# A two-layer graph kernel on Trainium2: the adjacency of layer 0 turned from the float32 tile itself, the first score pieces filled a round early, second buffers for two tiles

## The chip, the cores and the metric

The kernel runs on one core of one Trainium2 chip. The metric is device time in microseconds (us) of one execution. The kernel before took 15358.9 us, the median of three runs (15358.85 to 15360.56).

A core has five engines with an instruction queue each: PE (TensorE, matrix products; PEld is its loading of the stationary operand), DVE (VectorE), ACT (ScalarE), POOL (GpSimd) and SP (SyncE, which here only issues transfers). Sixteen DMA engines move data between device memory, SBUF (the on-chip memory, 128 partitions) and DRAM scratch. Matrix products land in PSUM.

## The reference

Two layers over 3327 nodes with 128 features, and a 0/1 adjacency matrix of 3327 x 3327 in float32. Both layers add their result to their input and normalize.

```python
# layer 0: cosine attention over the neighbours
norm2 = jnp.linalg.norm(x, axis=1, keepdims=True)
cos = beta[0] * (x @ x.T) / (norm2 @ norm2.T + 1e-07)
masked = cos + (1.0 - adj) * -1000000000.0
x = _layernorm(x + jax.nn.softmax(masked, axis=1) @ x)

# layer 1: 128 small attentions, one for each feature d, with 8 columns per head matrix
q = (x @ Wq.T).reshape(d, n, h); k = ...; v = ...
a = jnp.einsum('dnh,dmh->dnm', q, k) * scale
a = jax.nn.softmax(a + adj + adj, axis=2)
out = jnp.einsum('dnm,dmh->dnh', a, v).reshape(n, h * d) @ Wo.T
x = _layernorm(x + out)
```

## The kernel before

The nodes are padded to 3328 = 26 tiles of 128 rows (`T` = 26, `NP` = 3328). Layer 0 goes row tile by row tile and takes some 800 us; layer 1, the long part, takes the rest. In both, the order of PE, ACT, DVE and POOL is the order of the program text (a manual schedule), so that an instruction that has to wait holds up all that stands behind it on its engine. SP also issues its transfers in the order of the text.

**A tile's way through layer 0.** `load(t)` brings the adjacency rows as float32 into `u.raw` (1663.5 KB, through SP's queue; three buffers, shared with layer 1's keys) and the rows of x into `u.xr`. `load_bits(t)` brings the same rows a second time, through POOL's queue, converted to bf16 into `u.bits` (two buffers). `adj_chunk(t, c)` turns four 128 x 128 blocks of `u.bits` by matrix products with a unit matrix (L396) into a PSUM tile `tp`, and ACT copies them into `u.aT` (L397, one buffer); after the seventh chunk `u.aT` goes out to the scratch `aT_s` (L399), which layer 1 reads. `inverse_log`, `inverse_exp`, `inverse_product`, `inverse_newton` (L410, L417, L424, L431) make the reciprocals of the products of norms in `u.y`, on ACT and DVE. `mask(t)` (L403, ACT) turns the adjacency in `u.raw`, in place, into 0 or -1e9. `scores(t, j)` handles one of four pieces of 832 columns: `score_piece` fills a PSUM tile `sc` (two buffers) with x @ x.T (L359, four matrix products on record), then DVE scales it (L441) and adds the mask and takes the running minimum (L444). `weights(t, i)` (L460, ACT) takes the exponential of half a row. `turn_weights(t, c)` turns four blocks of it on PE (L134) into `tp` (two buffers, shared with `adj_chunk`) and copies them out (L474 on DVE, L472 on ACT for chunks 5 and 6); `weigh0` multiplies them with x (L482). `norm_begin`, `norm_root`, `norm_end` normalize. `project_turn` and `project(t, k)`, k = 0 to 5, make q, k and v of layer 1: each is a product into the PSUM tile `pq` (one buffer, L533) that ACT copies out, for q and k into `row` (L549), which POOL splits into `high` (L554) and `low` (L555), two buffers each, that go to scratch (L558, `qn_s` and `kn_s`); for v into `nine` (L535, one buffer), which goes to the scratch `v_s` (L539).

**A round.** The loop over t runs rounds -2 to 28, each with eight steps k = 0 to 7. Round t holds the scores of tile t (k = 0 to 3), the weights, turns and weighing of tile t-1, the normalization of tile t-2, the projections of tile t-3 (k = 0 to 4), the reciprocals and the mask of tile t+1 (k = 1 to 6), the turned adjacency of tile t+2 (chunk 0 at k = 4, chunks 1 and 2 at k = 5, 3 and 4 at k = 6, 5 and 6 at k = 7), `load(t + 3)` at k = 5, and `load_bits(t + 4)` at the end. After rounds 8, 12, 16 and 20 `gather` copies finished q and k rows from scratch to scratch. From round 26 on the first part of layer 1's search for row maxima is mixed in (`first_max`), and it uses the same two `sc` buffers.

The order at the head of a round, k = 0, is what the change touches on PE, ACT and DVE:

```python
weights(t - 1, 0)
project(t - 3, 0)
norm_begin(t - 2)
scores(t, 0)
turn_weights(t - 1, 0)
weights(t - 1, 1)
project(t - 3, 1)
norm_root(t - 2)
```

## Time and profile before

| what | us |
|---|---|
| median of three runs | 15358.9 |
| the profiled execution, its own time | 15361.32 |
| its span, first to last instruction | 15359.5 |
| layer 0, to the first product of layer 1's main loop | some 821 |
| PE / DVE / POOL / ACT busy in the whole span | 15192.6 / 13818.7 / 13765.0 / 12755.2 |

The profile is of one execution. Its page gives the busy time of each engine, the span in slices, the transfers by queue, the chain of waits that ended last, and the costliest groups of instructions. The trace behind it can be asked for any stretch: busy times and the granted clock of PE, the list of instructions in order of time with the idle time ahead of each and what ended it, and the sum of waits by who waited for whom. Times inside the span count from its first instruction. Of a matrix product the end is modelled, so neighbouring products overlap on record.

Where the rounds of layer 0 lie, by the start of their first scaling of scores (L441, in us; the list of instructions gives them):

| round | 0 | 1 | 2 | 3 | 4 | 5 | 11 | 13 | 15 | 19 | 23 | 25 |
|---|---|---|---|---|---|---|---|---|---|---|---|---|
| start | 62.1 | 78.2 | 101.6 | 123.7 | 149.2 | 174.3 | 322.8 | 376.3 | 430.7 | 538.4 | 647.0 | 696.1 |

From round 5 to round 11 a round takes (322.8 - 174.3) / 6 = 24.75 us, from 11 to 25 (696.1 - 322.8) / 14 = 26.66 us.

### The profile page before, as it was taken

To read this page: it belongs to the slowest core of one execution; us is meant where nothing else is said; L and a number is where in the kernel's file an instruction comes from. 1 tells how busy PE (TensorE), PEld (TensorE's weight loads), DVE (VectorE), ACT (ScalarE), POOL (GpSimd) and SP (SyncE) were. 2 spreads that over 40 slices of the span, in tenths; PEclk is the share of its full clock that TensorE was granted. 3 is DMA by queue.
4 is the path that set the end of the run, shared out by engine and by line. 5 is a ranking of instruction groups with operands and counts; after the bars stand their busy time and mean duration, and the time that the engine had idled before them with its cause. 6 is when DMAs were issued, how large, how long until landed. Compare 5 with 4: busy or idle time off the path is not lost.

```text
span 15359.5 us, 494776 instructions
## 1 busy us (share of the span) xinstructions
PE 15192.6 (99%) x210460; PEld 6695.5 (44%) x210460; DVE 13818.7 (90%) x15851; ACT 12755.2 (83%) x25413; POOL 13765.0 (90%) x8979
## 2 busy tenths in 40 slices
PE   8899999999999999999999999999999999999999
PEld 5534444444444444444444444444444444444555
DVE  7889999999999999999999999999999999998776
ACT  7689998888888888888888888888888888888777
POOL 3389999999999999999999999999999999998887
PEclk9999999999999999999999999999999999999999
DMA  7732221111111111111111111111111111111112
GB/s 229 226 103 97 101 98 60 48 51 48 56 50 47 52 53 53 46 53 46 60 47 53 47 58 48 51 48 55 51 46 53 46 59 46 53 46 62 62 59 83
DMA packets 553135, 1018.81 MB, mean 66 GB/s; under 512 B 148711, under 2 KB 493284, under 8 KB 504582
## 3 DMA queue, kind: packets, MB, share of 16 engines
q1 hardware_dynamic: 547126, 965.00, 19.1%
q0 software_dynamic: 3792, 22.15, 0.8%
q8 instruction: 1648, 27.00, 0.7%
q14 instruction: 569, 4.66, 0.1%
HBM read 871.04 MB, written 192.54 MB: 69 GB/s over the span
## 4 chain that ended last, share of the span: by engine, by line
PE 96%; DMA 1%; DVE 1%; ACT 1%; issue 0%; SPq 0%; POOL 0%; DVEq 0%; ACTq 0%; POOLq 0%
PE acc L808 30%; PE ea L778 22%; PE m L262 16%; PE eb L791 13%; PE ea L791 10%; PE ea L797 1%; PE ea L764 1%; DMA aT_s<-aT 1%; PE eb L797 1%; PE acc L482 0%; PE pq L533 0%; PE sc L359 0%; ACT aT L397 0%; PE pp L993 0%; DMA qn_s<-high 0%
## 5 line engine op out<-in xcount | busy, mean ns | idle before, releaser
L899 POOL TENSOR_TENSOR pb<-pb,eT 128x768 f32<-128x768 f32 (+1 forms) x7488 | 13175.3, 1767 | 980.4 <-ACT pb L898 594.0
L277 DVE TENSOR_REDUCE mx<-m 128x2 f32<-128x1024 f32 x6753 | 8275.0, 1225 | 958.6 <-PE eb L797 555.4
L898 ACT ACTIVATE pb<-eb 128x768 f32<-128x768 f32 (+1 forms) x7488 | 5898.0, 788 | 2255.7 <-PE eb L797 1731.1
L262 PE MATMUL m<-kn,qx 32*128 32x512 f32 (+1 forms) x23128 | 6804.0, 471 | 0.1
L922 ACT ACTIVATE pa<-ea 128x384 f32<-128x384 f32 (+1 forms) x14976 | 6338.9, 478 | 23.0 <-PE ea L778 8.4
L808 PE MATMUL acc<-pb,vt 128*9 128x384 f32 (+1 forms) x29952 | 5903.7, 474 | 0.1
L808 PE MATMUL acc<-pa,vt 128*9 128x384 f32 (+1 forms) x29952 | 5903.7, 474 | 0.0
L298 DVE TENSOR_REDUCE mx<-m 128x1 f32<-128x512 f32 x6371 | 4338.5, 681 | 252.0 <-PE m L262 232.3
L791 PEld LDWEIGHTS <-one 3*128 3x128 bf16 x29952 | 1465.8, 91 | 5659.0 <-issue 4661.4
L778 PE MATMUL ea<-aT,two 128*32 128x384 bf16 (+1 forms) x59904 | 3715.6, 325 | 0.0
L797 PE MATMUL eb<-qx,kn 32*128 32x384 f32 (+1 forms) x13312 | 3030.2, 451 | 0.0
L797 PE MATMUL ea<-qx,kn 32*128 32x384 f32 (+1 forms) x13312 | 2938.7, 433 | 0.0
L262 PEld LDWEIGHTS m<-kn,qx 32*128 32x128 f32 x23128 | 2797.6, 182 | 216.3 <-DVE mx L298 4.7
L791 PE MATMUL ea<-cx,one 3*128 3x384 bf16 (+1 forms) x14976 | 2724.4, 324 | 0.2
L791 PE MATMUL eb<-cx,one 3*128 3x384 bf16 (+1 forms) x14976 | 2466.1, 326 | 16.9 <-ACT cx L869 16.7
L808 PEld LDWEIGHTS acc<-pa,vt 128*9 128x9 f32 x29952 | 1418.2, 91 | 399.9
L808 PEld LDWEIGHTS acc<-pb,vt 128*9 128x9 f32 x29952 | 1418.6, 91 | 387.0 <-issue 0.7
L778 PEld LDWEIGHTS <-two 128*32 128x32 bf16 x59904 | 938.1, 94 | 1421.5 <-issue 1231.0
L797 PEld LDWEIGHTS eb<-qx,kn 32*128 32x128 f32 x13312 | 1275.0, 188 | 0.0
L797 PEld LDWEIGHTS ea<-qx,kn 32*128 32x128 f32 x13312 | 1237.0, 182 | 8.0 <-issue 1.3
L302 DVE TENSOR_REDUCE mx<-m 128x2 f32<-128x512 f32 x1084 | 739.7, 682 | 20.3 <-PE m L262 19.1
L554 POOL CAST high<-row 128x512 fp32r<-128x512 f32 x104 | 96.0, 923 | 328.7 <-DMA qn_s<-high 209.9
(134 smaller groups left out, 5972.2 us busy)
## 6 DMA issues: line engine op xcount, KB each, us to landing
kn<-kp_s SPq DMA_DIRECT2D x512, 832.0 KB
vt<-v_s SPq DMA_DIRECT2D x288, 409.5 KB
kn<-kq_s SPq DMA_DIRECT2D x64, 832.0 KB
qx<-qp_s SPq DMA_DIRECT2D x1016, 48.0 KB
kn<-in_adj_dram SPq DMA_DIRECT2D x25, 1663.5 KB
qp_s<-qn_s SPq DMA_DIRECT2D x64, 416.0 KB
kp_s<-kx SPq DMA_DIRECT2D x32, 832.0 KB
kq_s<-kn_s SPq DMA_DIRECT2D x64, 415.9 KB
```

What stands on the lines that cost most here:

```text
L262: nc.tensor.matmul(dst, u.qx[rows(a), q * P : (q + 1) * P], u.km[rows(a), k0:k1], start=True, stop=True,)
L277: nc.vector.tensor_reduce(u.mx[:, h, qs[0], c], m, axis=AX.X, op=ALU.max)
L298: nc.vector.tensor_reduce(u.mx[:, a, qs[0], c : c + 1], m, axis=AX.X, op=ALU.max)
L302: nc.vector.tensor_reduce(u.mx[:, a, qs[0] : qs[1] + 1, c], m.rearrange("p (q k) -> p q k", q=2), axis=AX.X, op=ALU.max,)
L764: nc.tensor.matmul(dst[r], parts[u.i % 2][:, q, h], unit, start=start, stop=True, tile_position=(0, 32 * h), skip_group_check=True,)
L778: nc.tensor.matmul(e[r, : u.nq], two[:, r], aT[:, j, : u.nq], start=False, stop=True, tile_position=(0, 32 * c), skip_group_check=True,)
L791: nc.tensor.matmul(e[:, : u.nq], one[r], u.cx[r, : u.nq], start=True, stop=False, skip_group_check=True)
L797: nc.tensor.matmul(e[:, : u.nq], u.kx[rows(a), j * P : (j + 1) * P], u.qx[rows(a), : u.nq], start=False, stop=stop, skip_group_check=True,)
L808: nc.tensor.matmul(acc[32 * h : 32 * h + H + 1, : u.nq], u.vt[:, h, j], pts[h][:, : u.nq], start=(j == 0), stop=(j == T - 1), tile_positio ...
L898: nc.scalar.activation(pt_b[:, :, : u.nq], e_b[:, :, : u.nq], AF.Exp)
L899: nc.gpsimd.tensor_tensor(pt_b[:, :, : u.nq], pt_b[:, :, : u.nq], eT[:, j, : u.nq].unsqueeze(1).to_broadcast([P, 2, u.nq]), ALU.mult,)
L922: nc.scalar.activation(pt_a[:, h, : u.nq], e[:, : u.nq], AF.Exp)
```

## The change

All of it is in layer 0.

- The second load of the adjacency is gone (`load_bits`, with its memset of the pad column and its transfer on POOL's queue, and the pool that held `bits`). `adj_chunk` reads instead the upper 16 bits of each float32 word of `u.raw`, which for 0 and 1 are the same number in bf16. Within a partition its 128 elements lie 104 bytes apart, those of `bits` lay 52 bytes apart. `u.raw` of tile t+2 must now be there at k = 4 of round t, before `mask(t + 2)` overwrites it in round t+1; before, it was first read at k = 4 of round t+1.
- `u.aT` has two buffers, and so has `nine`.
- The matrix products of `scores` move into `fill(t, j)`: pieces 0 and 1 of tile t+1 are filled at k = 6 and k = 7 of round t, ahead of the adjacency chunks of those steps; piece 2 at the end of k = 0, piece 3 at the end of k = 1. DVE's part of `scores(t, 0)` moves ahead of `project(t - 3, 0)` and `norm_begin(t - 2)`.

```diff
-        def load_bits(t: int):
-
-            u = tiles[t]
-            u.bits = adj_raw.tile([P, NP], BF16, name="bits", bufs=2)
-            load_adj(u.bits, nc.gpsimd, t)
+        def upper(t: int, k: int):
+
+            halves = tiles[t].raw.bitcast(BF16)
+            return halves.rearrange("r (p t h) -> r t h p", t=T, h=2)[:, k, 1, :]
 
         def adj_chunk(t: int, c: int):
...
-                u.aT = ptp.tile([P, T, P], BF16, name="aT", bufs=1)
+                u.aT = ptp.tile([P, T, P], BF16, name="aT", bufs=2)
...
-                nc.tensor.matmul(tp[:, k - a], every(u.bits, k), unit, start=True, stop=True)
+                nc.tensor.matmul(tp[:, k - a], upper(t, k), unit, start=True, stop=True)
...
+        def fill(t: int, j: int):
+            if there(t):
+                tiles[t].sc[j] = score_piece(xT[:, t * P : (t + 1) * P], xT, j)
+
         def scores(t: int, j: int):
...
-            sc = score_piece(xT[:, t * P : (t + 1) * P], xT, j)
+            sc = u.sc.pop(j)
...
             if n == 2:
+                nine = nines[t % 2]
...
-            for t in range(2):
-                load_bits(t)
-            nine = big.tile([P, P, R9], F32, name="nine")
-            nc.gpsimd.memset(nine[:, :, H], 1.0)
+            nines = [big.tile([P, P, R9], F32, name=f"nine{i}") for i in range(2)]
+            for nine in nines:
+                nc.gpsimd.memset(nine[:, :, H], 1.0)
...
                     if k == 0:
                         if there(t - 1):
                             weights(t - 1, 0)
+                        if there(t):
+                            scores(t, 0)
                         if there(t - 3):
                             project(t - 3, 0)
                         if there(t - 2):
                             norm_begin(t - 2)
-                        if there(t):
-                            scores(t, 0)
                         if there(t - 1):
                             turn_weights(t - 1, 0)
                             weights(t - 1, 1)
...
                             norm_root(t - 2)
+                        fill(t, 2)
...
                     if k < 5 and there(t - 3):
                         project(t - 3, k + 1)
+                    if k == 1:
+                        fill(t, 3)
+                    if k >= 6:
+                        fill(t + 1, k - 6)
                     if k == 5 and there(t - 2):
                         project_turn(t - 2)
...
-                if there(t + 4) and t + 4 > 1:
-                    load_bits(t + 4)
```

More of the change, by code (lines that the diff above doesn't have):

```diff
@@ L345, in gnn_two_layers @@
         big = l0.enter_context(tc.tile_pool(name="l0_big", bufs=1))
-        adj_raw = l0.enter_context(tc.tile_pool(name="adj_raw", bufs=2))
         work = l0.enter_context(tc.tile_pool(name="l0_work", bufs=2))
@@ L368, in gnn_two_layers, with there @@
         tiles = [Tile0() for _ in range(T)]
+        for u in tiles:
+            u.sc = {}
+        def there(n: int):
+            return 0 <= n < T
         half = NP // 2
@@ L633, in gnn_two_layers @@
             for t in range(-2, T + 3):
-                def there(n: int):
-                    return 0 <= n < T
                 for k in range(8):
```

## The prediction, on record before the change was run

> **What bounds the kernel now.** First the page's chain of waits, shares by engine and by line.

> ```profile
> PE 96%; DMA 1%; DVE 1%; ACT 1%; issue 0%; SPq 0%; POOL 0%; DVEq 0%; ACTq 0%; POOLq 0%
> PE acc L808 30%; PE ea L778 22%; PE m L262 16%; PE eb L791 13%; PE ea L791 10%; PE ea L797 1%; PE ea L764 1%; DMA aT_s<-aT 1%; PE eb L797 1%; PE acc L482 0%; PE pq L533 0%; PE sc L359 0%; ACT aT L397 0%; PE pp L993 0%; DMA qn_s<-high 0%
> ```

> 96% is PE, nearly all of it in layer 1, which the change leaves alone. Only layer 0, some 821 us or 5%, can move, and it ends before layer 1 begins, so what it saves passes to the end. The 1% of `aT_s<-aT` is about 114 us of chain, but not a gain of 114 us: while the chain goes through it, the rounds take nearly the usual time. So I went on by busy times, two stretches of 25 us (then narrow ones around a stall); the last two columns are the DMA engines' share and GB/s, and the one before them the granted clock.

> ```profile
> 212.90:237.70 24.80, 22.77 (x133) 15.88 (x133) 22.43 (x32) 20.38 (x28) 9.43 (x11) 1.00 0.86 250
> 395.00:420.00 25.00, 20.65 (x106) 13.69 (x106) 17.92 (x29) 16.70 (x22) 8.73 (x11) 0.93 0.77 233
> 575.30:578.70 3.40, 1.64 (x12) 1.22 (x10) 3.40 (x4) 0.89 (x2) 0.00 (x0) 1.00 0.97 403
> 578.70:582.10 3.40, 3.40 (x14) 2.24 (x14) 3.37 (x3) 3.14 (x2) 0.00 (x0) 0.51 0.80 272
> 237.40:240.80 3.40, 1.98 (x12) 1.34 (x11) 3.40 (x5) 3.37 (x2) 0.19 (x2) 1.00 0.55 160
> ```

> A quiet round (first line) is nearly full on PE, DVE and ACT at once, and the DMA engines are 86% busy. In a disturbed one the clock falls too: 3.4 us in which PE was busy 1.64 are followed by 3.4 us at half clock, 3.4 us with 1.98 are not. Next the sums of waits, and the queues, both from 95 to 700 us.

> ```profile
> POOL high L554 <- DMA qn_s<-high: 207.8, 19, 21.0
> DVE s L441 <- PE sc L359: 52.4, 40, 6.8
> ACT row L549 <- POOL low L555: 12.0, 3, 4.2
> ACT aT L397 <- DMA aT_s<-aT: 9.9, 8, 1.9
> ACT nine L535 <- DMA v_s<-nine: 9.4, 3, 4.1
> ...
> q1 hardware_dynamic: 110238, 127.12, 62.7%
> q0 software_dynamic: 3072, 17.89, 17.0%
> ```

> Three rows are ACT stopped by a transfer, 31.3 us: its tile is still going out, or POOL waits for its own. q0 is the load of `bits`: 17.0 of 79.7 points.

> **The second load and the second buffers.** The disturbed rounds are late by (26.66 - 24.75) x 14 = 26.7 us, which fits those 31.3 us, part of them absorbed, with the half clock behind them. With two buffers the rows of `aT` and `nine` go. The 12.0 us of `row` go if transfers keep up: q1 alone is 63%, and a round's raw load, v and turned tile queue up together from round 9 on only because each round was 80 to 90% full. I take 25 us off; bounds 19 (the two rows alone, all of it direct) and 31.

> **The start.** PE waits for x until 15.50, POOL until 19.83.

> ```profile
> 15.50 1.94 PE L134 MATMUL tp<-ident,xn 128*128 128x128 f32 x8 [15.50 <-DMA xn<-in_x_dram]
> 19.83 5.73 POOL L603 TENSOR_TENSOR s<-xn 128x3328 f32<-128x3328 f32 x1 [15.74 <-DMA xn<-in_x_dram]
> ...
> 2.00:7.00 5.00, 0.00 (x0) 0.00 (x0) 0.00 (x0) 0.02 (x1) 1.74 (x4) 1.00 0.88 249
> 7.00:14.00 7.00, 0.00 (x0) 0.00 (x0) 0.00 (x0) 0.00 (x0) 0.00 (x0) 1.00 1.07 241
> ```

> x's first transfer is 1638 KB; from 2 to 7 us it moves 249 x 5 = 1245 KB alone, then `bits` of two tiles shares the engines to 16 us. Without them the other 393 KB take 1.6 us, not 7: 5.3 us off, and all behind it moves up, the raw loads too (issued at 15.5, right after). Bounds 0 (another limit on x) and 9.5 (2 x 831.8 KB at that rate is 6.7, plus the wait behind them).

> **The scores filled early, first rounds.** In rounds 0 and 1 no projection fills PE, and DVE waits for `sc` 3.00, 2.22 and 0.59 us there. Filling early takes most of it, but at half clock a fill takes 2.8 us and now stands ahead of the adjacency chunks: 4 us off, bounds 0 and 6.

> **The scores filled early, a full round.** Here I follow one round by the step from one start to the next in the list of instructions from 195 to 222 us.

> ```profile
> 196.77 1.08 PE L533 MATMUL pq<-wq,x1T 128*128 128x512 f32 x2
> 197.36 1.69 ACT L460 ACTIVATE s<-s,mn 128x1664 f32<-128x1664 f32 x1
> 197.68 1.56 PE L359 MATMUL sc<-xT 128*128 128x416 f32 x4
> 199.19 0.66 PE L134 MATMUL tp<-ident,s 128*128 128x128 f32 x4
> 199.28 1.08 DVE L441 SCALAR_TENSOR_TENSOR s<-sc,by_q,y 128x832 f32<-128x832 f32 x1 [0.99 <-PE sc L359]
> 215.89 0.58 ACT L535 COPY nine<-pq 128x512 f32<-128x512 f32 x1
> 218.67 0.44 PE L134 MATMUL tp<-ident,s 128*128 128x128 f32 x2 [0.41 <-ACT aT L397]
> 220.29 1.95 ACT L397 CAST aT<-tp 128x512 bf16<-128x512 f32 x4 [0.78 <-PE tp L396]
> ```

> Let 196.77, PE's first projection, be 0. The first turn waits for ACT's weights: 0.6 (ACT ends its adjacency copies) + 1.69 + 0.13 = 2.4. Before, 1.4 us of scores stood in that wait; now nothing, so PE idles 1.3 to 1.5 us. From there PE's steps are projection 0.9, fill 1.4, turn 0.44, weighing 0.9, projection 0.86, fill 1.4, then (turn 0.44, weighing 0.9, projection 0.86) for k = 2 to 4. DVE comes before each of them now: its waits at the first and fourth turned block, 0.6 and 1.0 us, are gone. But ACT has 16.6 us of its own from the weights on: weights 3.5, logarithm 3.06, exponentials 3.1, mask 3.0, four rows and two v copies 3.0, the rest 0.9. With 0.6 ahead and 0.4 of waits its second v copy ends at 17.6; before it ended at 19.7. Then adjacency copy, weights copy, x1T and another adjacency copy, 1.75 together, let the seventh turn begin at 19.4; before 21.9, so 2.5 us gained. Behind it stand turn 0.28, weighing 0.9, fill 1.4, chunks 0.5, weighing 0.55, fill 1.4, chunks 0.6 = 5.6: the next round begins at 25.0, against 24.75. The fills leave the head, where they covered ACT, for the tail, where PE alone sets the pace; DVE gets 2 us of idle time that nobody uses. So +0.3 us a round for 23 rounds: +7. Bounds per round: -1.9 (DVE's busy 22.43 and small gaps, 22.85, if ACT could keep up) and +1.5 (no wait of DVE's was on the path).

> **What else moves.** The raw load is issued at 216.92, 20.2 us into its round, and now first read at adjacency chunk 0 of the next one, some 23 us later; in quiet rounds its packets are through 6 to 9 us after the issue, and PE would wait only if SP fell more than 14 us behind. Behind SP's load stand x's rows, the turned tile and the next `high`. In rounds 9 to 23 SP did issue it 8 to 13 us later in the round; that lag came with POOL's 207.8 us of waits for `high`. I put this at 0; the cover is those 14 us. The weight loads read words 104 bytes apart instead of 52. The trace has no such load; the nearest rows are PE's load of `bits` itself, 157 ns median with 83 ns from start to start, and ACT's copies at a step of 104 bytes (L752, 452 ns) against one without (L525, 266 ns). Bounds 0 and 0.19 x 26 = 4.8 us a round; I take 0, as PE's own row is nearer. POOL's memsets and issues, 0.7 us a round, stood in its idle time: 0.

> **Sum.** -25 - 5.3 - 4 + 7 = -27.3. The profiled execution took 15361.3 (span 15359.5), so 15334; it lies 2.4 above the median, so the median should come to **15332**.

> **Rivals.** *PE's new idle time halves its clock* (slower side). The place is the first turn of each round: 3.4 us with 1.64 busy us are punished, with 1.98 not. An idle 1.5 plus 0.1 at the next projection leaves 1.8, between them. It decides once the idle time passes 1.7, which a late adjacency copy of 0.2 us would do. A window of 3.4 us holds the whole gap in some 0.55 of rounds; half clock for one window costs 1.7 us, for two (as after 367 us) 3.4: 23 x 0.55 x 1.7 = +22, or 15354, and at two windows +43, or 15375, slower than before. Against it: gaps of 1.42 and 1.43 us in rounds 3 and 7 cost nothing. [...]

> *DVE sets the pace.* If ACT's copies slip into PE's idle time better than my steps let them, the round falls to 22.85: (24.75 - 22.85) x 23 = -44 instead of +7, so 15281. For it: 52.4 us of DVE waits named. Against: ACT's 16.6 us in the head leave no room.

> *The raw load comes late.* If SP's lag of 13 us stays, PE waits perhaps 2 us a round in 14 rounds and the 25 us come back: 15361. Against: with q0 gone the queue drains in each round.

> *The wide stride costs.* At half the bound, 2.4 x 26 = +62: 15394. Against: the loads of `bits` already skip.

> **How the numbers follow.** My forecast 0.56, half clock 0.21 (a fifth of it past 15390), DVE's pace 0.11, raw load 0.07, stride 0.05. The range for 8 in 10 goes from 15300, between the forecast and DVE's pace, to 15366, above the one-window clock case and the raw load; the likeliest case's own is 15318 to 15348. What a measurement can tell from no change is 0.2%, 31 us, so 15328 divides. Of the forecast 0.27 lies below it; with DVE's pace 0.38 faster. Slower, above 15390: 0.04 of the clock and 0.05 of the stride, 0.09. Within: 0.53.

> **What would show it.** Right: no q0 bytes in layer 0, x at PE near 10 us, waits of `aT` and `nine` for transfers gone, rounds from 11 to 25 as long as those from 5 to 11 and both near 25.0, DVE idle some 2 us more, the first turn waiting 1.3 to 1.5 us for the weights. Wrong: rounds at 23, a clock below 1.00 in quiet stretches, PE's chunk 0 waiting for a transfer, or weight loads over 160 ns.

## The result, and the profile after

| | us, median | range | runs |
|---|---|---|---|
| before | 15357.58 | 15354.04 to 15360.56 | 17 |
| changed | 15329.24 | 15327.57 to 15333.95 | 17 |

The changed kernel takes 0.9982 of the time before (95% interval 0.9974 to 0.9989): 28.3 us less. The profiled execution took 15328.18 us, its span is 15326.3; it lies 33.1 us under the profiled execution before, and the times by round below are of these two. One run of all that follow, 18264.56 us with the start moved, was in a slower state and is left out of that kernel's ratio.

The page's chain of waits, by engine and by line:

```profile
PE 94%; ACT 0%; issue 0%; DMA 0%; DVE 0%; POOL 0%; SPq 0%; ACTq 0%; DVEq 0%; POOLq 0%
PE acc L815 30%; PE ea L785 22%; PE m L262 16%; PE eb L798 13%; PE ea L798 10%; PE ea L804 1%; PE ea L771 1%; PE eb L804 1%; PE pp L1000 0%; ACT pa L929 0%; ACT oT L997 0%; PE otp L996 0%; DMA orow<-o_s 0%; ACT pb L905 0%; DMA kn<-kp_s 0%
```

The turned tile's transfer, 1% before, is gone from it. Next the busy times of two full rounds and of a long stretch (the last three columns are the granted clock, the share of the DMA engines and GB/s), the queues from 95 to 670 us, and the waits of the same stretch that answer to those shown before.

```profile
189.10:214.30 25.20, 22.30 (x138) 15.61 (x136) 22.30 (x33) 20.24 (x26) 9.71 (x9) 1.00 0.66 226
340.70:365.80 25.10, 22.19 (x136) 15.51 (x135) 22.20 (x33) 20.23 (x26) 9.69 (x9) 1.00 0.64 214
98.80:706.00 607.20, 543.90 (x3226) 378.90 (x3224) 541.75 (x760) 468.43 (x610) 260.31 (x214) 1.00 0.67 220
...
q1 hardware_dynamic: 110341, 125.90, 66.8%
...
POOL high L563 <- DMA qn_s<-high: 76.6, 10, 17.0
PEld tp L134 <- ACT s L468: 53.0, 22, 2.4
DVE pt L482 <- PE tp L134: 41.7, 24, 2.3
PE tp L134 <- ACT s L468: 37.3, 23, 2.5
DVE s L449 <- PE sc L358: 0.8, 2, 0.4
```

Three things are to be seen. The queue of the second load, 17 points, is gone, and the DMA engines are some 66% busy instead of 86%. DVE's wait for scores fell from 52.4 us to 0.8, but a wait of PE for the weights took its place, 37.3 us, and with it one of DVE for the turned block, 41.7. And the clock stays at 1.00 from 98.8 to 706 us, where before it fell to half eight times between 367.1 and 705.0 us.

Where the rounds lie now, by the start of their first scaling of scores (L449; L441 before), in us:

| round | 0 | 1 | 2 | 3 | 5 | 11 | 25 |
|---|---|---|---|---|---|---|---|
| before | 62.1 | 78.2 | 101.6 | 123.7 | 174.3 | 322.8 | 696.1 |
| changed | 51.3 | 67.4 | 90.0 | 114.1 | 164.0 | 315.5 | 664.2 |
| less | 10.8 | 10.8 | 11.6 | 9.6 | 10.3 | 7.3 | 31.9 |

So there is a gain of 10.8 us by round 0, a loss of 3 us from round 5 to 11 (25.25 us a round against 24.75), and a gain of 24.6 from 11 to 25 (24.91 against 26.66).

### The profile page after: what moved, and what is told of

Read it like the earlier page. It is cut to its first block, busy times and chain, and to the rows that moved or that the text cites. A ratio compares the mean times of both kernels' runs of the same rounds, so it can differ in the third digit from the quotient of the medians.

```text
span 15326.3 us, 494710 instructions
## 1 busy us (share of the span) xinstructions
PE 15162.1 (99%) x210460; PEld 6657.9 (43%) x210460; DVE 13818.2 (90%) x15851; ACT 12766.1 (83%) x25413; POOL 13781.4 (90%) x8926
## 3 DMA queue, kind: packets, MB, share of 16 engines
q1 hardware_dynamic: 547126, 965.00, 19.3%
## 4 chain that ended last, share of the span: by engine, by line
PE 94%; ACT 0%; issue 0%; DMA 0%; DVE 0%; POOL 0%; SPq 0%; ACTq 0%; DVEq 0%; POOLq 0%
PE acc L815 30%; PE ea L785 22%; PE m L262 16%; PE eb L798 13%; PE ea L798 10%; PE ea L804 1%; PE ea L771 1%; PE eb L804 1%; PE pp L1000 0%; ACT pa L929 0%; ACT oT L997 0%; PE otp L996 0%; DMA orow<-o_s 0%; ACT pb L905 0%; DMA kn<-kp_s 0%
## 5 line engine op out<-in xcount | busy, mean ns | idle before, releaser
L262 PE MATMUL m<-kn,qx 32*128 32x512 f32 (+1 forms) x23128 | 6788.7, 470 | 0.2 <-DVE mx L302 0.2
L262 PEld LDWEIGHTS m<-kn,qx 32*128 32x128 f32 x23128 | 2793.9, 181 | 230.1 <-DVE mx L298 6.3
L798 PE MATMUL eb<-cx,one 3*128 3x384 bf16 (+1 forms) x14976 | 2465.0, 326 | 16.8 <-ACT cx L876 16.6
```

The lines of the kernel that those rows point to most:

```text
L262: nc.tensor.matmul(dst, u.qx[rows(a), q * P : (q + 1) * P], u.km[rows(a), k0:k1], start=True, stop=True,)
L798: nc.tensor.matmul(e[:, : u.nq], one[r], u.cx[r, : u.nq], start=True, stop=False, skip_group_check=True)
```

## The experiments

Each kernel was run beside the kernel before; medians are of the runs shown with it (15358.78 us for the second load alone, the load with the second buffers, the fills alone and piece 1 in the head; 15359.67 for one buffer each, the start, the long rounds, and piece 1 in the head with four buffers; 15358.8 for the other two). The theory was that the second load costs the start and the crowding of the queue, the single buffers cost two waits of their own, and the early fills cost a little.

**The second load alone.** The kernel before, without `load_bits`, and with

```diff
-                nc.tensor.matmul(tp[:, k - a], every(u.bits, k), unit, start=True, stop=True)
+                nc.tensor.matmul(tp[:, k - a], upper(t, k), unit, start=True, stop=True)
```

> The kernel before with one part of the change: the second load of the adjacency is gone, the turning reads the upper halves of the raw tile; one buffer each for the turned tile and v, the scores filled in place. Theory (the second load costs the start and the crowding, the single buffers cost two waits of their own): the first scores begin some 8 us earlier than 62.1, quiet rounds stay at 24.75 us, the waits of ACT for the turned tile and for v, 19.3 us before, stay in part, and the time is 12 to 25 us under the kernel before (ratio 0.9984 to 0.9992). Rival (crowding alone made those waits): they vanish with one buffer each, rounds 11 to 25 fall to 24.75 us on average, and it is 33 to 37 us under (0.9976 to 0.9979), below the changed kernel.

Measured: 15329.48 us (15324.62 to 15335.49), ratio 0.9982 (0.9973 to 0.9990), 29.3 us less: all that the whole change brought, and between the theory's 12 to 25 and the rival's 33 to 37. ACT has no wait for the turned tile or for v any more, although each has one buffer; in that the rival is right. Two details fit neither side. Quiet rounds take 24.3 us, not 24.75. And two rounds, behind the gathers of rounds 16 and 20, still take 29.1 and 30.7. The list of instructions after the second of these gathers shows why (SP's issues, then ACT):

```profile
564.12 0.74 SPq L153 DMA_DIRECT2D kq_s<-kn_s  x1
...
566.83 0.59 SPq L154 DMA_DIRECT2D kq_s<-kn_s  x1
...
574.56 7.90 SPq L556 DMA_DIRECT2D qn_s<-high  x1
...
588.94 0.60 ACT L547 ACTIVATE row<-pq 128x512 f32<-128x512 f32 x1 [3.91 <-POOL low L553]
```

The gather's transfers go out at 564 to 567 us, right behind the raw tile, v and the turned tile. The parts of q stand behind them: one issue takes 7.90 us, POOL has no free buffer, and ACT at last waits 3.91 us for POOL.

**Second load and second buffers, without the fills.** The changed kernel with the scores filled in place as before.

> The changed kernel without its early fills: second load gone, two buffers each, scores filled in place as before. Theory (the early fills cost 0.35 us in each of some 22 full rounds and save 3 us in the first two): quiet rounds of 24.75 us, rounds 11 to 25 of 24.7 us on average, no wait of ACT for the turned tile or for v, and 4 us faster than the changed kernel, so 33 to 37 us under the kernel before (ratio 0.9976 to 0.9979). Rival (the early fills save DVE's waits for scores, 2.2 us a round): 20 us or more slower than the changed kernel, ratio 0.9994 or above.

15329.58 us (15326.87 to 15336.72), ratio 0.9981 (0.9972 to 0.9990). The rounds are those of the kernel without the second load: 24.3 us, with two long ones of 29 us at the same places. With the second load gone, the second buffers change nothing. The rival of 20 us falls, and so does the theory's 4 us for the fills in sum.

**One buffer each again, all else as changed.**

```diff
-                u.aT = ptp.tile([P, T, P], BF16, name="aT", bufs=2)
+                u.aT = ptp.tile([P, T, P], BF16, name="aT", bufs=1)
...
-                nine = nines[t % 2]
+                nine = nines[0]
...
-            nines = [big.tile([P, P, R9], F32, name=f"nine{i}") for i in range(2)]
+            nines = [big.tile([P, P, R9], F32, name=f"nine{i}") for i in range(1)]
```

> The changed kernel with one buffer again for the turned tile and for v. Theory (with the second load gone, the transfers of both are through before the next round writes them, as in the run without fills): no wait of ACT for them, rounds as in the changed kernel, ratio to the kernel before 0.9982 within 0.0003. Rival (the second buffers took away the waits): the 19.3 us of waits of the kernel before come back, 10 to 20 us slower than the changed kernel, 0.9988 or above.

15331.75 us (15328.32 to 15337.76), ratio 0.9982 (0.9973 to 0.9991), with no wait of ACT for either transfer. With the second load gone the second buffers have no use. The kernel before with the second buffers alone was not run, so whether they would have been enough beside the second load stays open.

**The fills alone.** The kernel before with `fill` and the new order at the head of a round.

> The kernel before with the early fills alone: second load kept, one buffer each. Theory: the first scores some 2 us early, quiet rounds 25.1 instead of 24.75 us, the turn at the head of a round waiting about 1.5 us for the weights, the waits of ACT for transfers about as before; within 8 us of the kernel before, rather slower (ratio 0.9998 to 1.0005). Rival (DVE's waits were the path): 25 to 45 us faster (0.997 to 0.9984).

15365.07 us (15362.09 to 15371.7), ratio 1.0004 (0.9995 to 1.0013). It is 6.3 us more, inside the 8 that were allowed, and the ranges of the two kernels overlap (before: up to 15364.35). The rival of 25 us and more is out. PE waits for the weights as in the changed kernel. With the second load kept there are still long rounds: 14, 18 and 22 take 33 to 35 us, where six of the kernel before take 28 to 31. The quiet rounds fit less well: 25.6 to 25.9 us in rounds 3 to 5, not 25.1.

**The start alone.** The kernel before with the first two second loads issued later:

```diff
-            for t in range(2):
-                load_bits(t)
...
             nc.gpsimd.tensor_mul(xs, xn, xn)
+            for t in range(2):
+                load_bits(t)
```

> The kernel before with one thing moved: the second loads of the first two tiles are issued behind POOL's squares of x instead of ahead of them, all later second loads stay. Theory (at the start x shares the transfer engines with those loads): POOL's squares begin at 12 us instead of 19.8, the first scores near 54.3 instead of 62.1, rounds from there on as before, so 7 to 8 us faster (ratio 0.9995). Rival (x is late for another reason): squares near 19, within 2 us.

15353.95 us, 5.7 less, ratio 0.9995 (0.9986 to 1.0004); the interval is wider than the step, so the time alone doesn't settle it. The list of instructions does:

```profile
12.00 5.73 POOL L601 TENSOR_TENSOR s<-xn 128x3328 f32<-128x3328 f32 x1 [10.05 <-DMA xn<-in_x_dram]
...
18.08 0.74 POOL L96 DMA_DIRECT2D bits<-in_adj_dram  x1 [0.31 <-POOL bits L94]
19.25 0.55 POOL L96 DMA_DIRECT2D bits<-in_adj_dram  x1 [0.31 <-POOL bits L94]
```

POOL begins at 12.00 us instead of 19.83, with the two loads merely moved behind it, and the first scaling at 53.6 instead of 62.1. The start was late because of the transfers that shared the engines with x.

**The long rounds.** The kernel without the second load, with four buffers for the parts of q and k:

```diff
-            high = ptp.tile([P, 512], F32R, name="high")
-            low = ptp.tile([P, 512], F32R, name="low")
+            high = ptp.tile([P, 512], F32R, name="high", bufs=4)
+            low = ptp.tile([P, 512], F32R, name="low", bufs=4)
```

> The kernel with the second load gone and nothing else changed, with four buffers each instead of two for the high and low parts of q and k. Theory (what is left of the long rounds, 29.1 and 30.7 us behind the gathers of rounds 16 and 20, is POOL waiting for a buffer whose transfer stands behind the gather and the raw tile): no wait of ACT for POOL, both rounds at 24.3 to 25 us, no half clock there, 9 to 12 us faster than that kernel, ratio to the kernel before 0.9974 to 0.9977. Rival (the queue is too full whatever the buffers): the rounds stay at 28 or more, or the wait moves to another transfer.

15319.47 us (15318.9 to 15325.12), ratio 0.9974 (0.9964 to 0.9984), 10 us under the kernel without them. All rounds from 3 to 23 take 24.3 to 24.8 us, ACT has no wait for POOL, and the granted clock of a full round (188.80 to 213.10 us) is 1.00. So more of these buffers are enough to end the last long rounds, with nothing taken from the queue.

**The fills, with nothing in the way.** The changed kernel with one buffer for the turned tile and v and four for the parts; against the kernel just above it differs by the fills alone.

> The changed kernel with one buffer each for the turned tile and v and four for the high and low parts of q and k; against the run with the second load gone and those four buffers it differs by the early fills alone, with no transfer in the way of either. Theory (the early fills cost a full round 0.8 us, 25.1 against 24.3, and save 3 us at the start): 13 to 17 us slower than that run, ratio to the kernel before 0.9983 to 0.9987, so four buffers bring the changed kernel nothing. Rival (the fills cost nothing, and the changed kernel's rounds are long for its transfers): within 5 us of that run, 0.9974 to 0.9978.

15334.99 us (15332.93 to 15336.82), ratio 0.9985 (0.9976 to 0.9994): 15.5 us more than without the fills, as the theory has it. Every run of the one lies above every run of the other. Every full round takes 25.1 us against 24.3, 0.8 x 22 = 17.6. The theory's 3 us at the start do not last: 2.6 by round 0 (51.4 against 54.0) are lost by round 3 (116.4 against 115.3). The fills by themselves make the kernel slower; that is measured here, where neither kernel has a long round.

**A fill put into the idle time.** The changed kernel with piece 1 filled in the head of its own round:

```diff
                         if there(t - 3):
                             project(t - 3, 0)
+                        fill(t, 1)
...
-                    if k >= 6:
-                        fill(t + 1, k - 6)
+                    if k == 6:
+                        fill(t + 1, 0)
```

> The changed kernel with one product moved: piece 1 of a tile's scores is filled in the head of its own round, behind the first projection, where PE waits 1.5 us for the weights, instead of at k = 7 of the round before. Theory (the round is one loop of ACT's head and PE's tail, and that wait is free time): the wait falls from 1.5 us to 0.1 or 0.2, the tail is 1.4 us shorter, a full round takes 23.7 us instead of 25.1, and the time is 25 to 32 us under the changed kernel (ratio to the kernel before 0.9962 to 0.9967). Rival (PE has no free time, or DVE or ACT sets the pace): rounds of 24.8 us or more, within 8 us of the changed kernel.

15308.01 us (15306.55 to 15310.72), ratio 0.9967 (0.9955 to 0.9980), 21 us under the changed kernel, not 25 to 32. The rounds did what was forecast, 23.4 to 23.8 us, but three long ones came back behind the gathers, 28.1, 28.8 and 27.4 us, with these waits from 95 to 670 us:

```profile
POOL high L563 <- DMA qn_s<-high: 132.0, 12, 19.0
ACT row L558 <- POOL low L564: 8.1, 3, 3.0
```

The wait for the parts' buffers is longer again than in the changed kernel (132.0 us against 76.6), and ACT waits for POOL; that shorter rounds leave the queue less time would fit. With one buffer each for the turned tile and v, and four for the parts:

> The changed kernel with piece 1 filled in the head of its round, as in the run that did this alone, with one buffer each for the turned tile and v and four for the high and low parts of q and k. Theory (its rounds of 23.4 to 23.8 us leave three rounds of 27 to 29 us behind the gathers, for want of those buffers): those fall to some 23.5 us, and it is 12 to 15 us faster than the run before it, ratio 0.9957 to 0.9960. Rival (rounds that short leave the queue no time, or the single buffers now wait): no faster than 0.9965.

15303.2 us (15301.64 to 15305.02), ratio 0.9962 (0.9949 to 0.9976): every round from 4 to 24 takes 23.8 or 23.9 us. This is the fastest version, 56.5 us under the kernel before and some 26 under the changed one. The gain over the run before it is 4.8 us, not 12 to 15, so that expectation was too high: round 25 begins 8.7 us earlier (634.7 against 643.4), and layer 1's main loop 9.2 us earlier (762.4 against 771.6), but the two profiled executions end only 6.0 us apart. The other 3 us go in layer 1, which is the same in both; why stays open.

**Another fill into the idle time.** The run with all fills and four buffers, but with `fill(t, 2)` moved up to stand behind `project(t - 3, 0)`.

> As the run before, but piece 2 of the scores is filled in the head, behind the first projection, instead of behind the second one; pieces 0 and 1 stay at the end of the round before. Theory (that fill uses the wait for the weights, but ACT's own work in the head then sets the pace and the tail keeps both fills): the wait at the first turn falls to 0.1 or 0.2 us, rounds of 24.1 us, 20 to 24 us faster than the run before, between it and the run with piece 1 in the head. Rival (only PE counts): rounds of 23.7 us as with piece 1.

15342.9 us (15341.02 to 15344.62), ratio 0.9990 (0.9981 to 0.9999): 8 us slower, where 20 to 24 faster was forecast. Both theories fall. The list of instructions of one round:

```profile
195.21 0.66 PE L134 MATMUL tp<-ident,s 128*128 128x128 f32 x4 [0.18 <-ACT s L468]
...
195.97 0.69 DVE L482 COPY pt<-tp 128x512 f32<-128x512 f32 x1 [2.18 <-PE tp L134]
...
204.86 2.17 DVE L452 CUSTOM_DVE_ANT_0 s<-s,kn,mn 128x832 f32<-128x832 f32 x1
204.88 1.27 POOL L564 TENSOR_TENSOR low<-row,high 128x512 fp32r<-128x512 f32 x1
...
207.69 1.16 PE L490 MATMUL acc<-xn,pt 128*128 128x128 f32 x8 [1.46 <-DVE pt L482]
```

PE's wait for the weights did fall to 0.18 us. But DVE, done with its part of piece 0, still waits 2.18 us for the first turned block, since that block comes no earlier; from there on DVE's own chain seems to set the pace: its fourth minimum takes 2.17 us beside POOL instead of 1.08, and PE waits 1.46 us for the fourth weighing. Rounds take 25.5 us. With piece 1 in the head, one fill leaves the tail; with piece 2, both stay.

## Why the prediction held, and where its reasons did not

It said 15332 against 15329.24 measured, so the sum was right, but in part by luck. Load and buffers were put at -30.3 us, start included, and brought 29.2 (the run with both and no fills). The fills were put at +7 - 4 = +3 us and cost 15.5 where nothing else is in the way; in the changed kernel that price is made up by two things that the prediction did not have, which are told behind the full round.

**The start** was mis-sized: 5.3 us were forecast, POOL's squares came 7.8 us earlier.

```profile
9.55 1.94 PE L134 MATMUL tp<-ident,xn 128*128 128x128 f32 x8 [9.55 <-DMA xn<-in_x_dram]
12.05 5.73 POOL L611 TENSOR_TENSOR s<-xn 128x3328 f32<-128x3328 f32 x1 [9.87 <-DMA xn<-in_x_dram]
```

The working looked at x's first transfer, for which PE waited (15.50, now 9.55: 6.0 us). The chain goes through POOL, which also needs the last rows of x; their transfer stood behind and gained 7.8 us. The first rounds gave another 10.8 - 7.8 = 3.0 us by round 0 and 3.8 by round 2, where 4 was forecast; 2 us of it went again in round 2, 24.1 us instead of 22.1. So the start gained more than forecast, and the first rounds less.

**The disturbed rounds** came out near the forecast, but "With two buffers the rows of `aT` and `nine` go" was the wrong step. The rows go without the second buffers, and the buffers added to that bring nothing (15329.58 against 15329.48). With one buffer each and no second load ACT waits for neither transfer, so taking away the crowding is enough. The prediction counted the single buffer, on which the wait is booked, as a cause of its own. From round 11 to 25 a round fell from 26.66 to 24.91 us, 24.5 us in all, where -25 and +0.3 x 14 make 20.8.

**A full round** was forecast at 25.0 us and takes 25.1. The step through it held nearly row by row:

```profile
191.58 1.08 PE L541 MATMUL pq<-wq,x1T 128*128 128x512 f32 x2
192.40 1.69 ACT L468 ACTIVATE s<-s,mn 128x1664 f32<-128x1664 f32 x1
194.24 0.66 PE L134 MATMUL tp<-ident,s 128*128 128x128 f32 x4 [1.58 <-ACT s L468]
208.71 0.58 ACT L544 COPY nine<-pq 128x512 f32<-128x512 f32 x1
208.81 0.66 PE L134 MATMUL tp<-ident,s 128*128 128x128 f32 x4 [0.61 <-DVE pt L482]
211.40 0.44 PE L134 MATMUL tp<-ident,s 128*128 128x128 f32 x2 [0.43 <-ACT aT L401]
```

From the first projection the first turn starts at 2.66 us (forecast 2.4), the second v copy ends at 17.7 (17.6), the seventh turn starts at 19.8 (19.4). But DVE does not come before each of PE's steps, as the prediction had it: PE waits 0.61 us for a copy of DVE's at 208.81 and 0.28 at 205.94. Nor is DVE idle 2 us more, but 0.5 (25.10 - 22.20 = 2.9 us a round, before 24.80 - 22.43 = 2.4).

What failed besides is what it was held against: without the second load, and with the scores in place, a round takes 24.3 us, not 24.75, so the fills cost 0.8 us and not 0.3. Some 0.4 us of this lie in DVE's work behind the fourth piece of scores, which takes longer beside POOL's; in the kernel before:

```profile
207.54 0.61 POOL L554 CAST high<-row 128x512 fp32r<-128x512 f32 x1 [3.17 <-DMA qn_s<-high]
...
210.80 1.27 POOL L555 TENSOR_TENSOR low<-row,high 128x512 fp32r<-128x512 f32 x1
211.48 1.47 DVE L444 CUSTOM_DVE_ANT_0 s<-s,kn,mn 128x832 f32<-128x832 f32 x1
```

and in the kernel without the second load:

```profile
200.05 1.28 POOL L553 TENSOR_TENSOR low<-row,high 128x512 fp32r<-128x512 f32 x1
201.27 1.08 DVE L442 CUSTOM_DVE_ANT_0 s<-s,kn,mn 128x832 f32<-128x832 f32 x1
```

Before, POOL was late with the parts of k, since it waited 3.17 us for a buffer, and its fourth subtraction fell on DVE's minimum, which took 1.47 us; without the load POOL is nearly through in time. It is not always this instruction: in round 8 the minimum began first and took 1.08 us, but POOL's subtraction then took 2.14, and DVE's product of the reciprocals (L424) right behind took 2.35 us instead of 1.94. In rounds 5 to 8 of the kernel before, the fourth minimum and that product together are 0.64, 0.39, 1.04 and 0.41 us longer than without the second load, and these rounds are 0.67, 0.43, 1.07 and 0.44 us longer than 24.35.

The changed kernel pays for such overlaps too, with POOL's copy or its subtraction: in its rounds of 25.1 us the third and fourth minimum take 1.40 and 1.38 us and the product 2.35. In its round 13 they take 1.08, 1.08 and 1.94, PE has no wait for DVE, and the round takes 24.6. So some 0.5 of the 0.8 us may be this, and not the fills' place at the end of the round. That the overlap is the cause is read from these traces; no run isolates it.

So the whole change gained no more than the second load alone, 28.3 us against 29.3. The fills lose some 15 us. 10 of them come back since no long round is left: ACT has no wait for POOL in the changed kernel, while without the fills two long rounds of 29 to 31 us remain, which four buffers showed to be worth 10 us. With the second load gone and two buffers for the parts, rounds of 23.8 us leave three long ones, rounds of 24.3 two, and rounds of 25.1 none; that longer rounds let the queue run empty after a gather would fit, but is not shown by itself. The other 5.7 us lie between it and the run with all fills and four buffers (15334.99); 3.2 of them come in rounds 13 to 24, which take 24.87 us on average against 25.13 there. Take the long rounds away by other means, and the fills show their price.

**The rivals.** Half clock at the head of each round did not come. From round 3 on PE waits 1.57 to 1.59 us there and the clock stays at 1.00 (in round 2, behind a wait of 2.49 us, it fell once, from 95.35 to 98.77), though in the kernel before it fell behind a gap of 1.37 us, the one ahead of 578.45. Of the stretches of 3.41 us that the changes of the clock mark off, the one around the wait at 469.79 has 1.82 us of PE's busy time (467.41 to 470.82), the one around that gap 1.65 (575.33 to 578.74). So the length of a gap alone does not part the two; that the busy time of the stretch does would fit, but is not shown by itself. DVE's pace of 22.85 us was never the pace of rounds in a row: with piece 1 in the head they take 23.4 to 23.8 us, and only single rounds just ahead of a long one take 22.3 to 22.6. The raw load comes in time: it is issued some 20.6 us after a round's first scaling, at 310.99 and 336.15 us in rounds 10 and 11 of the changed kernel, and PE waits for no transfer there. The wide stride costs nothing here: the weight loads at 104 bytes take 147 ns in the median, those at 52 bytes took 157.

## What to carry to other kernels

A wait that is booked on a single buffer may belong to the queue in front of it: ask what else is in the queue before adding a buffer, and try the two apart. Work moved out of an engine's wait is not free where it lands; look first at what it covered. A known wait can be filled with work from the part of the round that sets the pace (piece 1), but not at will (piece 2). When two parts of a change cancel in the sum, only runs of each part alone show it.

## What the runs showed of the hardware

DVE's minimum over 832 columns takes 1.08 us alone, and POOL's subtraction 1.27; beside each other one of the two took longer, or both (1.39 and 1.93 us at 200.75 and 201.34 in the changed kernel, where POOL's copy of 0.61 us had begun at 200.65). Where POOL's subtraction began first and reached well into it, the minimum ended 0.88 us behind it: at 212.95 against 212.07 in the kernel before. In the run with piece 2 in the head, where both begin within 0.02 us, it is 207.03 against 206.15. Where the minimum began first, the subtraction took 2.14 us (round 8 of the kernel before). So a delay of POOL became one of DVE, 1.47 us instead of 1.08, and where the third and fourth minimum took 1.39 and 1.38 us in the changed kernel, PE then waited 0.28 us for DVE (205.94).
